# A two-layer block on one core: the first group's work first, token normalisation on ScalarE, and a planner that counts changes of use of TensorE's array

## The chip, the cores and the metric

The kernel runs on one core of one Trainium2 chip. The core has five engines with their own instruction streams: TensorE (PE in the profile, with its weight loads as PEld), VectorE (DVE), ScalarE (ACT), GpSimd (POOL) and SyncE (SP), which issues the transfers. The metric is the device time of one execution in microseconds (us), taken as the median of the runs shown.

## The reference

Input x is 8 x 512 tokens of 256 values. Everything is float32. The first layer is

```python
xn = layernorm(x)                                   # over 256, eps 1e-5
x = x + attention(xn) + experts(xn)
```

with, for 16 heads of 64,

```python
q, k, v = rmsnorm(xn @ Wq) * qw, rmsnorm(xn @ Wk) * kw, xn @ Wv
gate = softplus(einsum(k, u / norm(u)) / 8)                      # one number per key and head
bias = -max(i - j, 0) * softplus(omega) * slope * gate[j]        # causal: -inf for j > i
y = softmax(q @ k.T / 8 + bias) @ v @ Wproj
```

and an expert layer in which each of 32 experts chooses 8 of the 512 tokens of a batch row (softmax over the tokens, top 8), merges them by their weights, applies 257 -> 1024 -> gelu -> 1025 -> 256, and adds the result back to its tokens. The second layer is

```python
xn = layernorm(x)
x = x + gelu(xn @ W_K.T @ W1.T) @ W2.T + ffn(xn)    # ffn: router picks 4 of 16 blocks of 64, relu
```

## The kernel before

**Work.** Attention runs in 32 groups (8 batch rows x 4 sets of four heads). A group is made by `produce(n)`: for each of four token tiles of 128, `project` computes q and k together (`q_k`, L597, 128x512 out), the values with four columns that give the gate's logit (`val`, L605, 260 columns), the square, sum and inverse root for the norm (L612, L629, L205), the scaled rows (L639) and their transposes (L655, L660, L667). After the fourth tile `gate` computes the softplus by a series of some 17 small VectorE steps (L698 to L710), splits the result into three bf16 parts on GpSimd (L730 to L751) and transposes it (L768, L775). Then eight units `attend(u)` run on the group: a unit is a pair of heads and one tile of query rows. Its `scores` (L807, L811) contract over 64 rows, so that two heads stand in the two halves of the array; then come the maximum (L820), the exponential (L828), the inverse (L835), the division on GpSimd (L838), the transposes (L851) with their copies (L859, L861), and after four units the `values` (L885), which use the array in two column halves. `output` (L915) multiplies a batch row's finished heads by Wproj. `expert` works on 4 experts at a time, in column quarters of the array (L992, L1052). `second` is the second layer, which runs for 8 batch rows at the end.

**Start.** `norm_rows(b)` loads a batch row of tokens, takes mean and variance (L408, L410), the inverse root on GpSimd (L414), normalises (L417), and transposes (L425) into `xnT`. Row 0 goes in four tiles, the others whole. `masks` and `bias_rows` (L236, L244) write two constant arrays on GpSimd that every score needs. `gate_weights(g)` (L340) multiplies Wk by the normalised vectors u of a set of heads, which gives the four extra columns of `val`. `choose` picks the experts' tokens for four batch rows. All loads stand on SyncE's queue.

**The order.** The program is written as a list of operations (`op`), each with its engine, an estimated cost in ns, what it depends on, a due time (`prio`, in units of attention: unit u is due at u) and counted buffers that it takes and gives back (`acq`, `rel`): two score buffers `sc`, two projection buffers `mm`, two transpose buffers `tr`, and so on. `Plan.emit` (L67) simulates the engines with these costs and writes out each engine's instructions in the order that it finds. On every engine it takes, among the operations due within the next 12 units, the first in due time that can start now, or else the one that can start earliest. An operation on TensorE has a `mode`, its use of the array: F (whole), R (two row halves: scores), C (two column halves: values), E (column quarters: experts), G and Q (small ones). The plan adds 93 ns where the mode differs from the last (L113); the mode has no part in the choice. The order is fixed when the program is built; on the chip the engines only wait for each other's semaphores.

```python
                    if ok and (pick is None or start < pick[0] - 1e-6):
                        pick = (start, o)
                        if start <= free[e]:
                            break
```

Of the kernel before, what the change touches and what calls it, by code (L numbers as in the profile page):

```python
# [15 lines left out]
P = 128  # L16
# [32 lines left out]
class Plan:  # L49
# [3 lines left out]
    SWITCH = 93  # L53
# [13 lines left out]
    def emit(self):  # L67
# [13 lines left out]
        while left:  # L81
# [4 lines left out]
            for e, ops in ready.items():  # L86
                pick = None
                for o in ops:
# [15 lines left out]
                    if ok and (pick is None or start < pick[0] - 1e-6):  # L104
                        pick = (start, o)
                        if start <= free[e]:
                            break
                if pick and (best is None or pick[0] < best[0]):
                    best = pick
            start, o = best  # L110
            cost = o.cost
            if o.eng == "PE":
                cost += self.SWITCH * (o.mode != mode)  # L113
                mode = o.mode
# [21 lines left out]
    AHEAD = 12.0  # L136


@with_exitstack
def tile_two_layer_block(  # L140
# [82 lines left out]
    with tc.tile_pool(name="pb", bufs=2) as pb, tc.tile_pool(name="pb1", bufs=1) as pb1:  # L223
# [20 lines left out]
        def bias_rows():  # L244
            nc.gpsimd.iota(bst, pattern=[[0, NPR], [1, T]], base=-MID, channel_multiplier=0,
                           allow_small_or_imprecise_dtypes=True)

            for h in range(2):
                k = slice(h * D, (h + 1) * D)
                for q in range(NPR):  # L250
                    r0 = 2 * NSP * q
                    for first, fill in ((r0 + NSP, 1.0), (r0 + 2 * NSP, 0.0)):
                        nc.gpsimd.affine_select(
                            out=bst[k, q, :], in_=bst[k, q, :], compare_op=ALU.is_ge, fill=fill,
                            base=first - 1, pattern=[[0, T]], channel_multiplier=-1,
                        )
                    if q:
                        nc.gpsimd.affine_select(
                            out=bst[k, q, :], in_=bst[k, q, :], compare_op=ALU.is_ge, fill=0.0,
                            base=-r0, pattern=[[0, T]], channel_multiplier=1,  # L260
                        )

        consts = [op("POOL", 2000, masks, (), -8.0), op("POOL", 5500, bias_rows, (), -7.0)]
        zeros = op("POOL", 2000, lambda: nc.gpsimd.memset(mT, 0.0), (), 4.0)

        def load(dst, src, prio, cost=60, acq=()):
            return op("DMA", cost, lambda: nc.sync.dma_start(dst, src), (), prio, acq=acq, lat=2000)
# [3 lines left out]
        for g in range(NHG):  # L271
            at = -18.0 if g == 0 else -9.0 + g
            w_qk[g], w_v[g] = [], []
            heads = slice(g * GW, (g + 1) * GW)
            for dc in range(NC):
                rows = slice(dc * P, (dc + 1) * P)
                w_qk[g].append(load(wqk_sb[:, dc, g, GW:], wk[rows, heads], at, 655))
            for dc in range(NC):
                rows = slice(dc * P, (dc + 1) * P)
                w_qk[g].append(load(wqk_sb[:, dc, g, :GW], wq[rows, heads], at + 0.1, 655))  # L280
                w_v[g].append(load(wvg_sb[:, dc, g, :GW], wv[rows, heads], at + 0.2, 655))
# [4 lines left out]
            load(w128[h * D : (h + 1) * D, k : k + 1], r.unsqueeze(1), -15.5)  # L286
# [34 lines left out]
        for k, f in enumerate(log1p_steps(lambda: oz, lambda: oy, lambda: oy2, lambda: om_sb)):  # L321
# [12 lines left out]
        v_u = [  # L334
            load(ub, u.rearrange("h d -> (h d)").partition_broadcast(P), -19.0, 600, acq=["eh"]),
            load(kwb, k_rms_w.partition_broadcast(P), -18.9, acq=["gT"]),
        ]
        w_g = {}

        def gate_weights(g, at):  # L340
            m = Grp()
            mine = ub3[:, g * HG : (g + 1) * HG, :]
            wide = lambda k: wqk_sb[:, k, g, GW:].rearrange("p (h d) -> p h d", d=D)

            def squares():
                m.sq = pb.tile([P, 2 * HG, D], F32, tag="sq", name=f"usq_{g}", bufs=1)
                nc.vector.tensor_mul(m.sq[:, :HG], mine, mine)

            def norms():
                m.un = pb.tile([P, HG], F32, tag="un", name=f"un_{g}")  # L350
                nc.vector.tensor_reduce(m.un, m.sq[:, :HG], AX.X, ALU.add)

            def floor():
                nc.vector.tensor_scalar(m.un, m.un, U_EPS, None, ALU.max)

            d = [op("DVE", 334, squares, v_u, at, acq=["sq"])]
            d = [op("DVE", 334, norms, d, at + 0.01)]
            d = [op("POOL", 1030, lambda: nc.gpsimd.tensor_tensor(m.un, m.un, phalf, ALU.pow),
                    d, at + 0.02)]
            d = [op("DVE", 86, floor, d, at + 0.03)]  # L360
            d = [op("DVE", 86, lambda: nc.vector.reciprocal(m.un, m.un), d, at + 0.04)]
            d = [op("DVE", 334, lambda: nc.vector.tensor_mul(
                mine, mine, m.un.unsqueeze(2).to_broadcast([P, HG, D])), d, at + 0.05)]
            d = [op("DVE", 334, lambda: nc.vector.tensor_mul(
                mine, mine, kwb.unsqueeze(1).to_broadcast([P, HG, D])), d, at + 0.06)]
            done = []
            for dc in range(NC):
                a = op("DVE", 334, lambda dc=dc: nc.vector.tensor_mul(
                    m.sq[:, dc * HG : (dc + 1) * HG], wide(dc), mine), d + w_qk[g], at + 0.07)
# [706 lines left out]
        for n in range(NIT):  # L1076
            produce(n)
            for k in range(NU):
                attend(n * NU + k)
# [531 lines left out]
```

## Time and profile before

| | us |
|---|---|
| median of 3 runs (1490.54 to 1491.31) | 1491.2 |
| the profiled execution | 1489.48 |
| its span, first to last instruction | 1487.8 |
| first score (L807) | 63.45 |
| last score | 1202 |
| TensorE idle in the span | 57.0 |
| ScalarE on exponentials (L828) | 284.2 |
| GpSimd on divisions (L838) | 266.2 |

The first 63 us bring in tokens and weights and make the first group; up to about 1204 us attention, outputs and experts share the engines; then the second layer follows. A group of instructions is named by its line, its engine and what it writes and reads; `x4` is a count. A releaser in brackets, such as `<-DVE x L417`, is what ended the engine's idle time just before. A matmul's duration includes the filling of the array, which overlaps the next one, so the distance of two starts says what it costs.

### The profile page before, as it was taken

The page shows a single profiled execution, that of the slowest core. Times are in us where ns is not written, and L with a number is a line of the kernel's source. Part 1 is how long each engine was busy: PE and PEld are TensorE (multiplying, and loading weights), DVE is VectorE, ACT ScalarE, POOL GpSimd, SP SyncE. Part 2 cuts the span into 40 slices and gives each one's busy share as a digit, 9 for nine tenths or more (in the row PEclk, how much of TensorE's full clock was granted, in tenths as well). Part 3 has the DMA queues.
Part 4 walks back from the last instruction along what each step waited for, and adds up shares of the span by engine and source line. Part 5 has one row for each costly group of instructions (what it writes and reads, how often), then busy time and mean ns, then how long its engine had stood idle before and what let it go on. Part 6 is the DMA issues. An engine that isn't in the chain of part 4 may idle for free.

```text
span 1487.8 us, 25107 instructions
## 1 busy us (share of the span) xinstructions
PE 1430.8 (96%) x8317; PEld 866.3 (58%) x8332; DVE 906.4 (61%) x3461; ACT 715.0 (48%) x1928; POOL 600.4 (40%) x1109
## 2 busy tenths in 40 slices
PE   3999999999999999999999999999999899999999
PEld 1555556556655665566556655665566466566666
DVE  6888776676677667766776677667766632322210
ACT  1455555555555556555655565655554531222221
POOL 5544554454454345444454454445444421111100
PEclk9999999999999999999999999999999999999999
DMA  6010111232231321232132213122220000000000
GB/s 203 4 57 1 61 61 60 73 111 65 81 102 59 103 85 57 63 105 80 58 118 65 65 62 114 65 69 85 79 74 9 1 15 15 11 18 15 19 15 22
DMA packets 74688, 90.19 MB, mean 61 GB/s; under 512 B 5800, under 2 KB 57760, under 8 KB 74560
## 3 DMA queue, kind: packets, MB, share of 16 engines
q1 hardware_dynamic: 74560, 88.59, 18.4%
q8 instruction: 67, 1.10, 0.3%
q14 instruction: 61, 0.50, 0.1%
HBM read 84.11 MB, written 4.19 MB: 59 GB/s over the span
## 4 chain that ended last, share of the span: by engine, by line
PE 86%; DVE 8%; ACT 3%; issue 1%; POOL 1%; DMA 1%; SPq 0%; ACTq 0%; DVEq 0%; POOLq 0%
PE pq L597 14%; PE pp L851 9%; PE y L885 8%; PE sc L811 8%; PE ph L1497 8%; PE py L1544 7%; PE po L915 7%; PE pv L605 7%; PE pqk L655 4%; PE sc L807 4%; PE peo L1052 2%; PE ph L992 2%; DVE pr L820 1%; ACT pr L828 1%; DVE ss L629 1%
## 5 line engine op out<-in xcount | busy, mean ns | idle before, releaser
L838 POOL TENSOR_SCALAR pr<-pr,rinv 128x384 f32<-128x384 f32 (+3 forms) x512 | 266.2, 533 | 324.9 <-DVE rinv L835 243.2
L828 ACT ACTIVATE pr<-pr,nm 128x384 f32<-128x384 f32 (+3 forms) x512 | 284.2, 557 | 112.6 <-DVE nm L820 72.8
L205 POOL TENSOR_TENSOR rsqk<-ss,nhalf 128x8 f32<-128x8 f32 x128 | 210.6, 1646 | 218.2 <-DVE ss L632 199.0
L820 DVE CUSTOM_DVE_ANT_0 pr<-sc,later 128x384 f32<-128x384 f32 (+3 forms) x512 | 238.8, 483 | 39.1 <-PE sc L811 35.7
L597 PE MATMUL pq<-wqk_sb,xnT 128*128 128x512 f32 x512 | 248.4, 608 | 2.6 <-DVE gl L623 2.6
L851 PE MATMUL pp<-ident,pr 128*128 128x128 f32 x1280 | 220.0, 282 | 10.6 <-POOL pr L838 2.8
L851 PEld LDWEIGHTS pp<-ident,pr 128*128 128x128 f32 x1280 | 149.7, 141 | 128.6 <-issue 67.8
L811 PE MATMUL sc<-kT,qT 64*128 64x384 f32 (+3 forms) x1024 | 181.9, 437 | 0.0
L859 ACT COPY prT<-pp 128x384 f32<-128x384 f32 (+3 forms) x256 | 107.6, 423 | 147.3 <-PE pp L851 146.4
L861 DVE COPY prT<-pp 128x384 f32<-128x384 f32 (+3 forms) x256 | 124.2, 486 | 72.1 <-PE pp L851 68.4
L885 PE MATMUL y<-prT,v 128*64 128x512 f32 (+3 forms) x1024 | 152.9, 439 | 2.2 <-ACT prT L859 1.8
L605 PE MATMUL pv<-wvg_sb,xnT 128*128 128x260 f32 x512 | 138.3, 393 | 2.3 <-DVE tm L639 2.3
L597 PEld LDWEIGHTS pq<-wqk_sb,xnT 128*128 128x128 f32 x512 | 88.5, 193 | 78.2 <-issue 67.1
L612 ACT ACTIVATE sq<-pq 128x512 f32<-128x512 f32 x128 | 76.2, 595 | 113.9 <-PE pq L597 98.9
L885 PEld LDWEIGHTS y<-prT,v 128*64 128x64 f32 x1024 | 69.1, 136 | 96.4 <-issue 65.3
L1497 PE MATMUL ph<-xT,mT 128*128 128x512 f32 x256 | 121.1, 595 | 0.6 <-DVE nm L820 0.2
L915 PE MATMUL po<-wp_sb,yT 128*128 128x256 f32 x512 | 116.1, 380 | 0.1
L629 DVE TENSOR_REDUCE ss<-sq 128x8 f32<-128x512 f32 x128 | 87.0, 680 | 37.8 <-ACT sq L612 37.5
L605 PEld LDWEIGHTS pv<-wvg_sb,xnT 128*128 128x128 f32 x512 | 89.6, 192 | 32.3 <-issue 9.4
L639 DVE TENSOR_TENSOR tm<-pq,rsqk 128x512 f32<-128x512 f32 x128 | 87.8, 686 | 31.7 <-POOL rsqk L205 30.8
L915 PEld LDWEIGHTS po<-wp_sb,yT 128*128 128x128 f32 x512 | 95.1, 190 | 13.0 <-issue 0.3
L1552 DVE TENSOR_TENSOR ot<-py,x 128x256 f32<-128x256 f32 x32 | 13.6, 424 | 143.7 <-PE py L1544 143.7
(259 smaller groups left out, 1885.4 us busy)
## 6 DMA issues: line engine op xcount, KB each, us to landing
ew<-in_L_ffn_w_dram SPq DMA_DIRECT2D x128, 512.0 KB
xr<-in_L_attn_x_dram SPq DMA_DIRECT2D x32, 128.0 KB
out_dram<-ot SPq DMA_DIRECT2D x32, 128.0 KB
x<-in_L_attn_x_dram SPq DMA_DIRECT2D x7, 512.0 KB
raw<-in_L_ffn_w_dram SPq DMA_DIRECT2D x4, 512.0 KB
wqk_sb<-in_L_attn_Wk_dram SPq DMA_DIRECT2D x8, 128.0 KB
wqk_sb<-in_L_attn_Wq_dram SPq DMA_DIRECT2D x8, 128.0 KB
wvg_sb<-in_L_attn_Wv_dram SPq DMA_DIRECT2D x8, 128.0 KB
```

The lines of the kernel that those rows point to most:

```text
L205: nc.gpsimd.tensor_tensor(r, src, nhalf[:, :n], ALU.pow)
L597: nc.tensor.matmul(s.pq[t], xnT[b][:, dc, cols], wqk_sb[:, dc, g, :], start=(dc == 0), stop=(dc == NC - 1),)
L605: nc.tensor.matmul(s.pv[t][:, : GW + HG], xnT[b][:, dc, cols], wvg_sb[:, dc, g, :], start=(dc == 0), stop=(dc == NC - 1),)
L811: nc.tensor.matmul(m.sc[:, h, :w], s.qT[k, q, n0:w], s.kT[k, q, :w], start=False, stop=True)
L820: nc.vector.tensor_tensor_reduce(m.p[:, h, :], m.sc[:, h, :w], later[:, T - w :], -1.0, BIG, ALU.add, ALU.min, m.nm[:, h : h + 1],)
L828: nc.scalar.activation(m.p[:, h, :], m.p[:, h, :], AF.Exp, bias=m.nm[:, h : h + 1], scale=-1.0, accum_out=m.sums[:, h : h + 1],)
L838: nc.gpsimd.tensor_scalar(m.p[:, h, :], m.p[:, h, :], m.rinv[:, h : h + 1], 1.0, ALU.mult, ALU.mult)
L851: nc.tensor.transpose(m.pt[h][:, d * P : (d + 1) * P], m.p[:, h, j * P : (j + 1) * P], ident)
L861: nc.vector.tensor_copy(dst, src)
L885: nc.tensor.matmul(pp.yp[h * D : (h + 1) * D, j * P :], s.v[j][:, hh * D : (hh + 1) * D], pp.tri[:, h, j : j + 4 * (NT - 1 - j) + 1 : 4, : ...
L915: nc.tensor.matmul(o.po[:, :C], yT[b * nk + k][:, t * P : (t + 1) * P], wp_sb[:, k, :], start=(k == 0), stop=(k == nk - 1),)
L1497: nc.tensor.matmul(m.ph[:, i, :], w1T[:, dc, k * P : (k + 1) * P], s.xT[:, dc, :], start=(dc == 0), stop=False,)
```

## The change

Six things change.

1. **The choice on TensorE.** `choose` in the plan takes, among the TensorE operations that can start at the earliest possible moment, the one with the least due time, after these shifts: one unit earlier for an operation with the mode in use, and for any other partial use after a partial use; one unit later for a score (R) after whole-array work when fewer than two R operations could start. The price of a changed mode is 96 ns, and 57 or 104 ns more on a return to the whole array (the second for an operation above 700 ns with the first price).
2. **First group first.** Wk, Wq and Wv of the first set of heads are loaded as whole transfers and early; Wv, u and the key norm's weights of this set go out on ScalarE's queue, and u is loaded by sets. An operation `begun`, which emits nothing, depends on everything that the first group's scores need; the other sets' gate weights, the statistics of batch rows 1 to 7 and the gate matrix of `choose` depend on it. The first group's q and k of two tiles use the score buffers, and its values the transpose buffers.
3. **Constants.** `bias_rows` no longer selects rows in 128x512 on GpSimd: two small tables of row scales are made there, and ScalarE writes each of the two arrays with one activation. Masks and tables come after the first roots. Zeroing of `mT` is cut in eight.
4. **Gate weights.** The square is ScalarE's, both halves of Wk are multiplied and summed in one step each, and the inverse norm is applied to the 8 results and not to u.
5. **Normalised tokens.** For batch rows 1 to 7 ScalarE applies scale and bias (28 steps of 128x256), with a bias that VectorE makes in one small step per row. Row 0 stays on VectorE.
6. **Due times and costs.** Rows 1 to 7 and `choose` are due later and further apart, experts start two groups of units later and follow each other in 6 instead of 6.5 units a quarter, and some estimated costs change (relu 675 for 485, q's copy 462 for 362, k's 394 for 334, the gate's 335 for 598).

```diff
     LAT = {"PE": 220, "DVE": 140, "ACT": 140, "POOL": 90, "DMA": 0}
-    SWITCH = 93
+    SWITCH = 96
+    SECOND = 57, 104
...
                 pick = None
+                able = []
...
-                    if ok and (pick is None or start < pick[0] - 1e-6):
+                    if ok and e != "PE" and (pick is None or start < pick[0] - 1e-6):
                         pick = (start, o)
                         if start <= free[e]:
                             break
+                    if ok and e == "PE":
+                        able.append((start, o))
+                if able:
+                    pick = self.choose(able, free[e], mode)
                 if pick and (best is None or pick[0] < best[0]):
                     best = pick
             start, o = best
             cost = o.cost
             if o.eng == "PE":
-                cost += self.SWITCH * (o.mode != mode)
+                if o.mode != mode:
+                    cost += self.SWITCH
+                    if o.mode == "F":
+                        cost += self.SECOND[cost > 700]
                 mode = o.mode
...
+    SAME, OTHER, ALONE = 1.0, 1.0, 1.0
+    def choose(self, able, free, mode):
+        now = max(free, min(s for s, _ in able))
+        can = [o for s, o in able if s <= now + 1e-6]
+        alone = mode == "F" and sum(o.mode == "R" for o in can) < 2
+        def due(o):
+            if o.mode == mode:
+                return o.prio - self.SAME
+            if "F" not in (o.mode, mode):
+                return o.prio - self.OTHER
+            return o.prio + self.ALONE * (alone and o.mode == "R")
+        best = min(can, key=due)
+        return now, best
...
+        pos = pb.tile([P, T], F32, tag="pr1", name="pos", bufs=1)
...
+        def row_scales():
+            nc.gpsimd.iota(pos, pattern=[[1, T]], base=-MID, channel_multiplier=0,
                            allow_small_or_imprecise_dtypes=True)
...
+        def bias_rows(q):
+            nc.scalar.activation(
+                bst[:, q, :], pos, AF.Identity, bias=rows[:, 1, q : q + 1],
+                scale=rows[:, 0, q : q + 1],
+            )
+        zeros = [
+            op("POOL", 270, lambda e=e: nc.gpsimd.memset(mT[:, :, e : e + 4, :], 0.0), (),
+               4.0 + 0.1 * e)
+            for e in range(0, E, 4)
+        ]
+        def load(dst, src, prio, cost=470, acq=(), by="DMA"):
+            go = nc.scalar if by == "ACT" else nc.sync
+            return op(by, 100 if by == "ACT" else cost, lambda: go.dma_start(dst, src), (), prio,
+                      acq=acq, lat=2000 + (cost if by == "ACT" else 0))
...
-            w_qk[g], w_v[g] = [], []
+            at = -23.5 if g == 0 else -9.0 + g
+            by = "ACT" if g == 0 else "DMA"
...
+            w_qk[g] = [
+                load(wqk_sb[:, :, g, GW:], both(wk), at, 900),
+                load(wqk_sb[:, :, g, :GW], both(wq), at + 0.1, 900),
+            ]
+            w_v[g] = [load(wvg_sb[:, :, g, :GW], both(wv), at + 0.2, 900, by=by)]
...
+        v_kw = load(kwb, k_rms_w.partition_broadcast(P), -23.8, acq=["gT"], by="ACT")
+        v_u = {}
+        for g in range(NHG):
+            v_u[g] = [v_kw, load(
+                ub[:, g * GW : (g + 1) * GW],
+                u[g * HG : (g + 1) * HG, :].rearrange("h d -> (h d)").partition_broadcast(P),
+                -23.9 if g == 0 else -9.1 + g, 500, acq=["eh"] if g == 0 else [],
+                by="ACT" if g == 0 else "DMA",
+            )]
         w_g = {}
+        roots = []
+        begun = op("POOL", 1, lambda: None, (), -6.9)
...
+            d = [op("ACT", 272, squares, v_u[g] + ([begun] if g else []), at, acq=["sq"])]
+            s = [op("DVE", 334, lambda: nc.vector.tensor_reduce(
+                m.un, m.sq[:, :HG], AX.X, ALU.add), d, at + 0.01)]
             d = [op("DVE", 334, lambda: nc.vector.tensor_mul(
-                mine, mine, m.un.unsqueeze(2).to_broadcast([P, HG, D])), d, at + 0.05)]
-            d = [op("DVE", 334, lambda: nc.vector.tensor_mul(
-                mine, mine, kwb.unsqueeze(1).to_broadcast([P, HG, D])), d, at + 0.06)]
-            done = []
-            for dc in range(NC):
-                a = op("DVE", 334, lambda dc=dc: nc.vector.tensor_mul(
-                    m.sq[:, dc * HG : (dc + 1) * HG], wide(dc), mine), d + w_qk[g], at + 0.07)
-                done.append(op("DVE", 334, lambda dc=dc: nc.vector.tensor_reduce(
-                    wvg_sb[:, dc, g, GW:], m.sq[:, dc * HG : (dc + 1) * HG], AX.X, ALU.add),
-                    [a], at + 0.08))
-            w_g[g] = done + [op("DVE", 1, lambda: None, done, at + 0.09,
-                                rel=["sq"] + (["eh", "gT"] if g == NHG - 1 else []))]
+                mine, mine, kwb.unsqueeze(1).to_broadcast([P, HG, D])), d, at + 0.015)]
+            r = [op("POOL", 1030, lambda: nc.gpsimd.tensor_tensor(m.un, m.un, phalf, ALU.pow),
+                    s, at + 0.02)]
+            roots.extend(r)
+            r = [op("DVE", 86, lambda: nc.vector.tensor_scalar(m.un, m.un, U_EPS, None, ALU.max),
+                    r, at + 0.03)]
+            r = [op("DVE", 86, lambda: nc.vector.reciprocal(m.un, m.un), r, at + 0.04)]
+            d = [op("DVE", 598, products, d + s + w_qk[g][:1], at + 0.07)]
+            d = [op("DVE", 598, lambda: nc.vector.tensor_reduce(
+                m.gw.rearrange("p k h -> p (k h)"), m.sq, AX.X, ALU.add), d, at + 0.08)]
+            w_g[g] = [op("DVE", 86, lambda: nc.vector.tensor_mul(
...
-            gate_weights(g, -17.0 if g == 0 else -3.0 + 2 * g)
+            gate_weights(g, -15.95 if g == 0 else -3.0 + 2 * g)
...
-                            [ld], a_)
+                            [ld] + ([begun] if b else []), a_)
...
+                if b == 0:
+                    roots.append(rs)
+                else:
+                    nb = op("DVE", 86, lambda t0=t0, t1=t1: nc.vector.scalar_tensor_tensor(
+                        m.ve[:, t0:t1], m.mv[:, t0:t1, 0], -1.0, m.rs[:, t0:t1],
+                        ALU.mult, ALU.mult), [rs], a_ + 0.04)
                 for t in ts:
-                    xn = op("DVE", 334, lambda t=t: nc.vector.tensor_scalar(
-                        m.x[:, t, :], m.x[:, t, :], m.mv[:, t, 0:1], m.rs[:, t : t + 1],
-                        ALU.subtract, ALU.mult), [rs], a_ + 0.1)
+                    if b:
+                        xn = op("ACT", 370, lambda t=t: nc.scalar.activation(
+                            m.x[:, t, :], m.x[:, t, :], AF.Identity, bias=m.ve[:, t : t + 1],
+                            scale=m.rs[:, t : t + 1]), [nb], a_ + 0.1)
+                    else:
+                        xn = op("DVE", 334, lambda t=t: nc.vector.tensor_scalar(
+                            m.x[:, t, :], m.x[:, t, :], m.mv[:, t, 0:1], m.rs[:, t : t + 1],
+                            ALU.subtract, ALU.mult), [rs], a_ + 0.1)
...
-        tg = op("PE", 150, turn_gw, [v_g], 4.0, acq=["tr"], mode="G")
+        tg = op("PE", 150, turn_gw, [v_g, begun], 4.0, acq=["tr"], mode="G")
...
+        first = roots[:1] + roots[-NT:]
+        consts = [op("POOL", 1000, masks, first, -8.0)]
+        sc_ = op("POOL", 2000, row_scales, first, -7.9, acq=["pr1"])
+        for q in range(NPR):
+            consts.append(op("ACT", 485, lambda q=q: bias_rows(q), [sc_], -7.0,
+                             rel=["pr1"] if q == NPR - 1 else []))
         for b in range(1, BPG):
-            norm_rows(b, 2.0 * b, [list(range(NT))])
-        choose(0, 8.0)
+            norm_rows(b, 5.0 * b, [list(range(NT))])
+        choose(0, 19.0)
         for b in range(BPG, B):
-            norm_rows(b, 10.0 + 2.0 * (b - BPG), [list(range(NT))])
-        choose(1, 18.5)
+            norm_rows(b, 21.0 + 4.0 * (b - BPG), [list(range(NT))])
+        choose(1, 38.0)
...
+                qk_in = "sc" if n == 0 and t < 2 else "mm"
+                v_in = "mm" if n else "tr"
...
-                a = op("PE", 1716, q_k, x_T[b] + w_qk[g], at + w, acq=["mm"])
+                a = op("PE", 1716, q_k, x_T[b] + w_qk[g] + vals[-2:-1], at + w,
+                       acq=[qk_in])
                 projected.append(a)
-                v = op("PE", 876, val, x_T[b] + w_v[g] + w_g[g], at + w + 0.01, acq=["mm"])
+                v = op("PE", 876, val, x_T[b] + w_v[g] + w_g[g], at + w + 0.01, acq=[v_in])
+                vals.append(v)
...
+            if n == 0:
+                begun.deps += grp[0].ready
...
-        step = (NIT - NHG - 2) * NU / (4 * NG)
+        step = (NIT - NHG - 4) * NU / (4 * NG)
         for g in range(NG):
-            h0, h1, d0, d1 = (NHG * NU + step * (4 * g + k) + 0.7 for k in range(4))
+            h0, h1, d0, d1 = ((NHG + 2) * NU + step * (4 * g + k) + 0.7 for k in range(4))
...
-                    hid.append(op("ACT", 485, lambda i=i, f=relu: f(i),
+                    hid.append(op("ACT", 675, lambda i=i, f=relu: f(i),
```

## What the change does to the time: a prediction

> **What bounds the kernel now.** I read the page's first part, then the chain of waits, then the busy time by stage, and last TensorE's own timeline.
>
> ```profile
> PE 1430.8 (96%) x8317; PEld 866.3 (58%) x8332; DVE 906.4 (61%) x3461; ACT 715.0 (48%) x1928; POOL 600.4 (40%) x1109
> ...
> PE 86%; DVE 8%; ACT 3%; issue 1%; POOL 1%; DMA 1%; SPq 0%; ACTq 0%; DVEq 0%; POOLq 0%
> ```
>
> TensorE is the bound: 1430.8 of 1487.8 us busy, and 86% of the chain that ended last. So only two things can shorten the run: TensorE's idle time (57.0 us) and time inside its "busy" that does no work. By stage (columns: length, then busy time and count of PE, PEld, DVE, ACT, POOL; clock; DMA share; GB/s):
>
> ```profile
> 0.00:63.45 63.45, 35.41 (x118) 19.99 (x119) 47.17 (x178) 13.52 (x31) 32.92 (x70) 0.92 0.41 122
> 63.45:200.00 136.55, 130.90 (x830) 74.80 (x831) 109.75 (x431) 77.38 (x229) 70.37 (x128) 0.99 0.13 43
> 200.00:1200.00 1000.00, 985.76 (x6126) 588.84 (x6128) 682.03 (x2583) 558.88 (x1563) 470.66 (x878) 1.00 0.22 72
> 1200.00:1487.80 287.80, 278.71 (x1249) 182.63 (x1258) 67.47 (x274) 65.26 (x108) 26.46 (x34) 0.99 0.05 17
> ```
>
> Idle: 28.0 us before the first score at 63.45, then 5.7, 14.2 and 9.1. Half of all idle time is in the first 4% of the run. No other engine passes 80% of a long stage after that.
>
> The start, from the timelines of GpSimd, VectorE and TensorE:
>
> ```profile
> 7.99 2.61 POOL L253 TENSOR_SCALAR_AFFINE_SELECT bst<-bst 64x512 bf16<-64x512 bf16 x4
> 11.36 1.02 POOL L358 TENSOR_TENSOR un<-un,phalf 128x4 f32<-128x4 f32 x1
> 12.36 2.08 POOL L414 TENSOR_TENSOR ars<-ave,nhalf 128x1 f32<-128x1 f32 x4
> 16.39 1.34 PE L425 MATMUL pxT<-ident,x 128*128 128x128 f32 x4 [16.39 <-DVE x L417]
> 32.13 0.69 PE L425 MATMUL pxT<-ident,x 128*128 128x128 f32 x2 [4.08 <-DVE x L417]
> 39.73 3.00 PE L597 MATMUL pq<-wqk_sb,xnT 128*128 128x512 f32 x4
> ```
>
> The token roots (L414) stand on GpSimd behind the constant rows, though their input is ready at about 4 us; TensorE first moves at 16.39. Later it waits 4.08 us for tokens of the second batch row, ahead of the first row's own second and third tile.
>
> A steady piece of TensorE's timeline (start, duration; the next start, not the duration, says what a row costs):
>
> ```profile
> 63.45 0.34 PE L807 MATMUL sc<-gT,bst 64*128 64x384 bf16 x2 [0.16 <-DVE gT L775]
> ...
> 64.26 0.23 PE L807 MATMUL sc<-gT,bst 64*128 64x128 bf16 x2
> ...
> 514.78 0.66 PE L851 MATMUL pp<-ident,pr 128*128 128x128 f32 x4
> 515.37 0.34 PE L807 MATMUL sc<-gT,bst 64*128 64x384 bf16 x2
> 515.54 0.81 PE L811 MATMUL sc<-kT,qT 64*128 64x384 f32 x4
> 516.28 0.66 PE L851 MATMUL pp<-ident,pr 128*128 128x128 f32 x4
> 516.77 1.88 PE L597 MATMUL pq<-wqk_sb,xnT 128*128 128x512 f32 x4
> 518.49 1.04 PE L605 MATMUL pv<-wvg_sb,xnT 128*128 128x260 f32 x4
> ...
> 532.25 0.60 PE L851 MATMUL pp<-ident,pr 128*128 128x128 f32 x4
> 532.69 0.64 PE L597 MATMUL pq<-wqk_sb,xnT 128*128 128x512 f32 x1
> ```
>
> Four transposes inside whole-array work take 0.44 (532.25 to 532.69); just after scores 0.49; just after column-tiled work and ahead of scores 0.59 (514.78 to 515.37). A 384-wide score takes 0.81 with another score behind it (63.45 to 64.26), 0.91 with whole-array work behind it. So leaving a use of the array costs 0.10, and coming back to the whole array 0.05 more; ahead of a projection it is 0.10 more (in that timeline pq takes 1.82 us after a score, 1.72 after transposes).
>
> **Part 1, the order (choose, SECOND).** Over the whole TensorE timeline I counted 662 changes of use and 297 returns to the whole array: 662 x 0.097 + 297 x 0.062 (mean of both return prices) = 83 us, 5.6% of the run. The 256 scores stand in 226 visits; only 30 visits hold two. A visit avoided saves 0.10 + 0.10 + 0.06 = 0.26 us. With two score buffers a visit can hold two. Is the second buffer free? A score is issued every 4.45 us (63.45 to 1204 us, 256 of them), and at 500 to 533 us VectorE has read a score 1.5 to 2.5 us after its issue, so both are free half the time; a lone score is held back one unit (4.45 us) while other work is there. The trace shows no order by this rule: bounds are no pair more (0) and all paired (98 visits x 0.26 = 25.5). I take four scores of five paired, 154 visits: 72 x 0.26 = **18.7**. Values and experts enter from the whole array 59 times; put behind a score they save 0.16 each; bounds 0 and 9.4, I take 24, **3.8**. Sum 22.5.
>
> What the moved work costs: a later score makes exponentials, divisions and transposes later, and the VectorE maxima come four in a row (up to 2.8 us by 0.69 us rows). Cover is the ready projections and outputs on TensorE; without it, every pair leaves a wait. That price is a rival below.
>
> The Trainium skill, page "TensorEngine Tiling (Array Packing)", section "Key Properties", says that a change of tiling mode drains the array but not a change of tile; it gives no time, and the 0.10 us above is this case's price. By that rule alone a switch between scores and values should cost as much as any other.
>
> **Part 2, the start.** First tokens land at 2.95 and their variances are ready at 3.97, as now. With the constant rows (7.6 us of GpSimd, 3.69 to 11.27) behind the roots: root 0.5, normalise 0.4, transpose 0.7, copy 0.4: first tile at 6.2. Weights: x 0.52, Wk, Wq, Wv 0.26 each, u 0.13, together 1.4 MB, at 167 GB/s (0 to 16.39 us) 8.6, at 253 GB/s (16.39 to 31.78) plus 2 us of latency 7.7; take 8. Then four tiles of 1.72 + 0.88 = 10.4, transposes between them 1.7, cold clock 2.7: 22.8 for the last tile, pq ending 0.9 earlier. Its square, sum, mean, root and gate scale are 0.60 + 0.68 + 0.17 + 1.65 + 0.17 = 3.3, 25.5 with hand-overs. The gate: 17 small VectorE steps 3.2, Exp 0.2, eight GpSimd steps 2.2, transpose 0.4, copy 0.4, hand-overs 0.8: 7.2. First score at 33 instead of 63.45. Bounds: 28 (no cold clock, no hand-overs), 38 (the gate as slow as now, 51.64 to 63.45).
>
> TensorE's useful work by then: 10.4 + token transposes 1.1 + q/k transposes 1.8 + 0.2 + two tiles ahead 3.4 = 16.9, so 16.1 us lost. Before: 28.0 idle and 6.3 of slow matmuls (pq 3.62 and 3.00 against 1.88, and five shorter rows), 34.3. Gain 18.2. Given back: the deferred gate weights and tokens meet the first scores on VectorE, and the pipeline fills with little else: between 0 and 10 (twice the 5.7 of 63 to 200), take 4.5. Net **13.5**, bounds 3 and 23.
>
> The clock row first: after the 4.08 us wait, slice 30 to 40 us had a granted clock of 0.59 and pq took 3.00. The page "TensorE: Matmul & The Clock Gate", section "What's actually happening", says that idling one window of about 3.4 us halves the clock until a busy window. By it the wait for the gate, which is new here ahead of the first score, brings one more cold window: 1.7 us, an estimate from that page; the sum would be 34.3 for 36. It speaks against the change.
>
> Against loads on ScalarE's queue the page "DMA: Bandwidth & Descriptors", section "Issuing engines are not separate DMA queues", says that only issue time is saved. The rows' 167 and 253 GB/s from one queue fit it.
>
> **Part 3, the rest.** Normalised tokens: 28 VectorE steps of 0.44 go (12 us), 7 of 0.17 come; ScalarE gets 28 of about 0.47 (the nearest row, L660, scaled 128x256; 0.37 by the plain copy) = 13 us. Cover: ScalarE is 52% idle and rows 1 to 7 have 19 units or more until use; without cover the loss is 28 x 0.03. Identity at L500 runs with no table load. The two bias-row steps on ScalarE (0.68 each by L500) and split zeroing lie before or beside scores: 0. Omega, norm weights and the later groups' loads are moved behind the first on SP; they are due after 9 us: 0. The tail from 1200 us: scores' rule also delays the 16 start steps; costs for relu are nearer the rows (0.68). Idle there is 9.1, so between -5 and +5; 0.
>
> **Sum.** 22.5 + 13.5 = 36.0. The profiled execution took 1489.48 (span 1487.8), 1.7 below the median 1491.2. 1489.5 - 36.0 = 1453.5, plus 1.7: **1455**.
>
> **Rivals.**
> 1. Few new pairs: one buffer is usually still held when a score falls due, and the one-unit delay rarely decides. Against: the 2 us hold in 4.45. Order gain 7, start 13.5: 1471.
> 2. The start gives it back: VectorE, 74% busy in the first 63 us, makes up the deferred work later and TensorE idles 10 instead of 4.5 us, with the first score at 38: start gain 3, order 22.5: 1466.
> 3. All pairs and joins come, first score at 28: 25.5 + 9.4 + 21: 1435.
> 4. Slower: pairs starve TensorE. For: transposes already wait up to 2.48 us for a division, and two transpose buffers serve scores, tokens, q/k and values. Place: the transposes (L851) after each pair. It decides from 36.0 / 128 = 0.28 us a pair; at 0.37 it costs 47: 1502. Against: 14.2 us idle in 1000 now, with work of twelve units to choose from.
>
> **How the numbers follow.** Chances: forecast 0.60 (1441 to 1466), few pairs 0.13, start given back 0.08, everything 0.07, slower 0.10, and 0.02 for effects that cancel. Range 1434 to 1483: the low end is rival 3, the high end an order gain of 6 and a start gain of 3. Runs of this kernel spread by 0.8 us, so 0.2% (3 us) is the bound for no change: faster 0.86, same 0.03, slower 0.11.
>
> **What would show it.** After: first score near 33 us; TensorE idle before it near 13; scores in about 154 visits; TensorE busy near 1405; idle in the attention stage still near 15 per 1000. Wrong if visits stay above 200, if the first score is later than 40, or if idle time ahead of L851 rises from 10.6 to over 40.

## The result and the profile after

The changed kernel took 1464.49 us (median of 4 runs, 1463.22 to 1464.89) against 1490.87 before: ratio 0.9828, 95% interval 0.9815 to 0.9841. It is 26.4 us faster; 36 were forecast. Over all comparisons single runs of the kernel before lie between 1486.3 and 1491.9 us, with medians from 1489.1 to 1490.9, so a difference of 2 or 3 us between kernels that were timed in different rounds is not certain. The page after, first part and chain:

```profile
PE 1414.9 (97%) x8332; PEld 866.3 (59%) x8332; DVE 888.8 (61%) x3428; ACT 735.0 (50%) x1961; POOL 595.7 (41%) x1115
...
PE 85%; DVE 7%; ACT 5%; issue 1%; POOL 1%; DMA 1%; ACTq 0%; SPq 0%; DVEq 0%; POOLq 0%
```

TensorE is busy for 15.9 us less with the same matmuls, and idle for 48.3 us instead of 57.0. By stage, with the same columns as above:

```profile
0.00:41.73 41.73, 23.05 (x76) 12.84 (x77) 23.57 (x91) 12.30 (x25) 22.05 (x70) 0.97 0.60 181
41.73:200.00 158.27, 151.32 (x908) 90.62 (x909) 129.56 (x531) 104.86 (x298) 86.76 (x146) 0.98 0.05 16
200.00:1200.00 1000.00, 984.18 (x6233) 599.00 (x6230) 677.99 (x2578) 562.63 (x1550) 467.01 (x874) 0.99 0.24 76
1200.00:1463.20 263.20, 256.34 (x1119) 163.86 (x1117) 57.63 (x231) 55.26 (x88) 19.88 (x25) 1.00 0.05 17
```

The first score starts at 41.73 instead of 63.45, with 18.7 us of idle time before it instead of 28.0. In the attention stage TensorE idles 15.8 us per 1000 instead of 14.2. TensorE's start:

```profile
10.04 1.11 PE L489 MATMUL pxT<-ident,x 128*128 128x128 f32 x4 [10.04 <-DMA w<-in_L_attn_q_rms_w_dram]
12.81 1.35 PE L489 MATMUL pxT<-ident,x 128*128 128x128 f32 x4 [1.65 <-issue]
13.95 3.62 PE L673 MATMUL pq<-wqk_sb,xnT 128*128 128x512 f32 x4
...
35.50 0.63 PE L731 MATMUL pqk<-ident,tm 128*128 128x128 f32 x4 [1.49 <-DVE gp L357]
39.24 1.08 PE L731 MATMUL pqk<-ident,tm 128*128 128x128 f32 x4 [3.12 <-DVE tm L715]
...
41.73 0.51 PE L886 MATMUL sc<-gT,bst 64*128 64x384 bf16 x2 [0.64 <-DVE gT L854]
42.00 1.51 PE L890 MATMUL sc<-kT,qT 64*128 64x384 f32 x4
```

The first projection (L673) starts at 13.95, behind the transposes of all four tiles. Before the first score TensorE waits for the gate, and the score then takes 1.51 us; 0.82 is usual. A pair of the changed order, at full clock:

```profile
53.93 0.28 PE L886 MATMUL sc<-gT,bst 64*128 64x256 bf16 x2
54.05 0.60 PE L890 MATMUL sc<-kT,qT 64*128 64x256 f32 x4
54.49 0.33 PE L886 MATMUL sc<-gT,bst 64*128 64x384 bf16 x2
```

Two scores follow each other, and the 256-wide one costs 0.56 (53.93 to 54.49) where a lone one took 0.65 before.

### The profile page after: what moved, and what is told of

It is laid out like the page before. It is cut to its first block, busy times and chain, and to the rows that moved or that the text cites. A ratio compares the mean times of both kernels' runs of the same rounds, so it can differ in the third digit from the quotient of the medians.

```text
span 1463.2 us, 25079 instructions
## 1 busy us (share of the span) xinstructions
PE 1414.9 (97%) x8332; PEld 866.3 (59%) x8332; DVE 888.8 (61%) x3428; ACT 735.0 (50%) x1961; POOL 595.7 (41%) x1115
## 4 chain that ended last, share of the span: by engine, by line
PE 85%; DVE 7%; ACT 5%; issue 1%; POOL 1%; DMA 1%; ACTq 0%; SPq 0%; DVEq 0%; POOLq 0%
PE pq L673 13%; PE pp L930 10%; PE sc L890 8%; PE y L964 8%; PE ph L1578 8%; PE po L994 8%; PE py L1625 7%; PE pv L681 7%; PE pqk L731 3%; PE sc L886 3%; PE peo L1131 2%; PE ph L1071 2%; ACT pr L907 2%; DVE pr L899 2%; PE ph L1582 1%
## 5 line engine op out<-in xcount | busy, mean ns | idle before, releaser
L907 ACT ACTIVATE pr<-pr,nm 128x384 f32<-128x384 f32 (+3 forms) x512 | 284.6, 557 | 142.6 <-DVE nm L899 116.1
L673 PE MATMUL pq<-wqk_sb,xnT 128*128 128x512 f32 x512 | 245.2, 602 | 0.3 <-DVE gl L699 0.2
L930 PEld LDWEIGHTS pp<-ident,pr 128*128 128x128 f32 x1280 | 151.2, 141 | 133.0 <-issue 78.8
L930 PE MATMUL pp<-ident,pr 128*128 128x128 f32 x1280 | 219.3, 281 | 10.7 <-POOL pr L917 3.4
L964 PE MATMUL y<-prT,v 128*64 128x512 f32 (+3 forms) x1024 | 154.1, 444 | 2.0 <-DVE kT L743 1.2
L673 PEld LDWEIGHTS pq<-wqk_sb,xnT 128*128 128x128 f32 x512 | 88.4, 192 | 73.1 <-issue 62.2
L964 PEld LDWEIGHTS y<-prT,v 128*64 128x64 f32 x1024 | 68.4, 138 | 95.7 <-issue 66.3
L1633 DVE TENSOR_TENSOR ot<-py,x 128x256 f32<-128x256 f32 x32 | 13.5, 423 | 157.6 <-PE py L1625 157.6
L715 DVE TENSOR_TENSOR tm<-pq,rsqk 128x512 f32<-128x512 f32 x128 | 87.9, 686 | 21.8 <-POOL rsqk L234 20.6
```

The lines of the kernel that those rows point to most:

```text
L673: nc.tensor.matmul(s.pq[t], xnT[b][:, dc, cols], wqk_sb[:, dc, g, :], start=(dc == 0), stop=(dc == NC - 1),)
L907: nc.scalar.activation(m.p[:, h, :], m.p[:, h, :], AF.Exp, bias=m.nm[:, h : h + 1], scale=-1.0, accum_out=m.sums[:, h : h + 1],)
L930: nc.tensor.transpose(m.pt[h][:, d * P : (d + 1) * P], m.p[:, h, j * P : (j + 1) * P], ident)
L964: nc.tensor.matmul(pp.yp[h * D : (h + 1) * D, j * P :], s.v[j][:, hh * D : (hh + 1) * D], pp.tri[:, h, j : j + 4 * (NT - 1 - j) + 1 : 4, : ...
```

## Experiments

Each kernel is the changed one with one edit, except `order_only`. "Changes" and "returns" are changes of use of the array and returns to the whole array, counted in each built program (before 658 and 296, changed 536 and 212; the trace of before, used in the prediction, gave 662 and 297). "Priced" is 0.097 us a change and 0.062 a return. Busy and idle are TensorE's in the profiled execution, which is one run and not always near the median: it took 1486.8 us for `start_only`, 1477.4 for `order_only`, 1478.3 for `same3` and 1475.1 for `partial1_whole3`.

| kernel | median us | ratio to before, 95% | visits of two scores | changes, returns | priced | busy | idle |
|---|---|---|---|---|---|---|---|
| before | 1490.9 | | 30 | 658, 296 | 82.2 | 1430.8 | 57.0 |
| changed | 1464.5 | 0.9815 to 0.9841 | 69 | 536, 212 | 65.1 | 1414.9 | 48.3 |
| order_only | 1480.3 | 0.9919 to 0.9943 | 68 | 530, 209 | 64.4 | 1415.0 | 60.7 |
| start_only | 1482.1 | 0.9944 to 0.9972 | 31 | 646, 289 | 80.6 | 1430.3 | 54.6 |
| norm_dve | 1466.1 | 0.9827 to 0.9853 | 67 | 538, 212 | 65.3 | 1413.8 | 49.9 |
| same3 | 1481.7 | 0.9926 to 0.9954 | 106 | 457, 172 | 55.0 | 1412.2 | 64.3 |
| partial0_whole1 | 1480.0 | 0.9933 to 0.9961 | 26 | 594, 227 | 71.7 | 1419.0 | 58.2 |
| partial1_whole0 | 1490.5 | 0.9997 to 1.0017 | 51 | 604, 262 | 74.8 | 1425.4 | 61.2 |
| partial3_whole1 | 1460.4 | 0.9798 to 0.9828 | 113 | 475, 196 | 58.2 | 1405.1 | 54.3 |
| partial1_whole3 | 1472.9 | 0.9876 to 0.9912 | 69 | 515, 192 | 61.9 | 1417.1 | 56.2 |
| own_tile | 1461.1 | 0.9801 to 0.9829 | 69 | 536, 212 | 65.1 | 1410.8 | 48.1 |
| no_gating | 1460.6 | 0.9800 to 0.9828 | 66 | 543, 216 | 66.1 | 1411.9 | 47.0 |
| old_due | 1470.6 | 0.9863 to 0.9892 | 64 | 538, 213 | 65.4 | 1415.2 | 52.2 |
| partial3_own_tile | 1458.0 | 0.9780 to 0.9808 | 113 | 475, 196 | 58.2 | 1404.6 | 52.0 |

### The order alone, and the rest alone

`order_only` is the kernel before with the new class `Plan`; `start_only` is the changed kernel with the old one.

```diff
 class Plan:
-    SWITCH = 93
+    SWITCH = 96
+    SECOND = 57, 104
...
+                if able:
+                    pick = self.choose(able, free[e], mode)
```

> The kernel before with the new choice and prices on TensorE alone. Its program has 530 changes of use and 209 returns to the whole array, before 658 and 296. Theory 1 (each change costs 0.097 us and each return 0.062 on the path): 128 x 0.097 + 87 x 0.062 = 17.8 us faster than before, about 1473; the start stays as before (first score near 63 us). Theory 2 (changes of use are hidden; the gain came from the start and the due times): within 3 us of before, 1488 to 1494. Theory 3 (pairing starves TensorE of transposes and only the start pays): slower than before.

> The changed kernel with the choice and the price of the kernel before, all else as changed. 646 changes and 289 returns, the changed kernel 536 and 212. Theory 1: 110 x 0.097 + 77 x 0.062 = 15.4 us slower than the changed kernel, about 1480; so the start, the due times and the rest are worth some 11 of 26 us. Theory 2: within 3 us of the changed kernel's 1464.5. Theory 3: faster than the changed kernel.

The order alone brings 10 us (1490.3 to 1480.3, the medians of that comparison), less than theory 1's 17.8; TensorE's busy time falls by 15.8, near its price, but its idle time rises by 3.7. Taking the order out of the changed kernel costs 17.6 us by the medians, a little more than the 15.4 of theory 1; the profiled run of `start_only`, 4.7 us above its median, has 15.4 more busy and 6.3 more idle. So theories 2 and 3 fall, and theory 1 comes near in one of the two kernels. The new prices were not tried apart from the new choice. The rest alone brings 8.2. The two alone make 18.2 of 26.4; 8 us come only with both.

### Keeping a use

```diff
-    SAME, OTHER, ALONE = 1.0, 1.0, 1.0
+    SAME, OTHER, ALONE = 3.0, 1.0, 1.0
```

> The changed kernel with the bonus for the use in force raised from 1 unit to 3 (SAME 3, OTHER 1, ALONE 1): 106 visits hold two scores instead of 69, 41 one instead of 118; 457 changes and 172 returns instead of 536 and 212. Theory 1: 79 x 0.097 + 40 x 0.062 = 10.1 us faster than the changed kernel, 1454 to 1455. Theory 3 (more pairs starve TensorE): not faster than 1464, and idle time of TensorE between 200 and 1200 us above 25 instead of 15.8.

17 us slower than the changed kernel, though it makes 79 changes fewer. In 200 to 1200 us TensorE idles 29.3 us instead of 15.8:

```profile
200.00:1200.00 1000.00, 970.74 (x6181) 597.42 (x6180) 671.38 (x2553) 550.22 (x1541) 464.99 (x870) 1.00 0.23 76
```

This fits theory 3. But SAME does two things: it keeps scores together, and it holds scores back behind whole-array work. The next four kernels set the two apart:

```diff
             if o.mode == mode:
-                return o.prio - self.SAME
+                return o.prio - (3 if mode != "F" else 1)
```

with the pairs (0, 1), (1, 0), (3, 1) and (1, 3) for a partial use and the whole array.

> The changed kernel with its bonus split by the use in force: none for staying in a partial use, 1 unit for staying with the whole array (so a score is only held back, and two are no longer kept together). 594 changes, 227 returns, 26 visits of two scores. Theory 1 (the count of changes sets the gain: start_only with 646 and 289 took 1482.1): 52 x 0.097 + 62 x 0.062 = 8.9 us faster than that, 1473. Theory 4 (holding scores back behind ready whole-array work is itself the gain, the pairs are by the way): 1463 to 1468.

> The other half: 1 unit for staying in a partial use, none for staying with the whole array. 604 changes, 262 returns, 51 visits of two scores. Theory 1: 42 x 0.097 + 27 x 0.062 = 5.7 us faster than start_only, 1476. Theory 4: no gain over start_only, 1480 to 1490.

> 3 units for staying in a partial use, 1 for the whole array: 113 visits of two scores (69 in the changed kernel), 475 changes, 196 returns (536, 212). Theory 1: 61 x 0.097 + 16 x 0.062 = 6.9 us faster than the changed kernel, 1457 to 1458. Theory 3 (pairs starve TensorE, as same3's 1481.7 may say): 1472 or more, and idle of TensorE in 200 to 1000 us near same3's 17.8 instead of 7.6. Theory 5 (same3 lost by staying too long with the whole array, pairs are harmless): 1457 to 1464.

> 1 unit for staying in a partial use, 3 for the whole array: 69 visits of two scores as in the changed kernel, 515 changes, 192 returns. Theory 1: 21 x 0.097 + 20 x 0.062 = 3.3 us faster than the changed kernel, 1461. Theory 5: slow like same3, 1475 or more. Theory 3: near the changed kernel, 1460 to 1466, since the pairs are the same.

`partial3_whole1` has more pairs than `same3` and is the fastest of the five. Its pairs cost some idle time in this stage (20.6 us for 15.8) and save more busy time (9.8 us over the run), so theory 3 falls. With 3 units for the whole array instead of 1 the kernel is slower twice (`same3` against `partial3_whole1`, `partial1_whole3` against the changed kernel), as theory 5 says, though its 1475 or more for the latter was missed. Its stage, then that of `partial1_whole3`, which has the changed kernel's pairs but stays long with the whole array:

```profile
200.00:1200.00 1000.00, 979.43 (x6249) 606.01 (x6249) 684.30 (x2574) 550.88 (x1547) 464.10 (x872) 1.00 0.23 76
```

```profile
200.00:1200.00 1000.00, 976.88 (x6184) 593.83 (x6182) 672.52 (x2569) 571.30 (x1554) 467.07 (x863) 0.99 0.23 75
```

20.6 and 23.1 us idle. The last is 8.4 us slower than the changed kernel where its count made it 3.3 faster.

The trace of `partial1_whole3` shows where: 10.4 of the 23.1 us are four waits of 2.61 us ahead of values. ScalarE has a table to load whenever it goes from the exponential (L907) to the experts' gelu (L1098) or back, 1.28 us each time. The plan counts one such load for the two gelu steps of an expert stage (`586 + 1283 * (1 - half)`). In the changed kernel the two stand together; here an exponential stands between them, which makes four loads instead of two, and the copy that the values need comes late:

```profile
402.45 1.28 ACT L1098 ACT_TABLE_LOAD   x1
403.74 1.15 ACT L1098 ACTIVATE ehT<-ehT 128x512 f32<-128x512 f32 x2
405.13 1.28 ACT L907 ACT_TABLE_LOAD   x1 [0.24 <-DVE nm L899]
```

```profile
397.44 0.63 ACT L1098 ACTIVATE ehT<-ehT 128x512 f32<-128x512 f32 x1
398.08 1.28 ACT L907 ACT_TABLE_LOAD   x1
...
399.87 1.28 ACT L1098 ACT_TABLE_LOAD   x1
401.17 0.63 ACT L1098 ACTIVATE ehT<-ehT 128x512 f32<-128x512 f32 x1
401.70 0.35 ACT L938 COPY prT<-pp 128x256 f32<-128x256 f32 x1
402.11 3.88 PE L964 MATMUL y<-prT,v 128*64 128x512 f32 x16 [2.61 <-ACT prT L938]
```

So the loss in this kernel is in large part ScalarE's order, and not, as theory 5 says, an array kept too long in one use. The two gelu steps are split in four expert stages here and in `partial0_whole1`, in two in `same3`, `order_only` and `old_due` (below), and in none of the others. No kernel that only joins them was run.

The two halves of the bonus alone gave 1480.0 and 1490.5, against 1464.5 with both and 1482.1 for `start_only`, which also lacks OTHER, ALONE and the new prices. The first fails theories 1 and 4; the second has no gain over `start_only`, as theory 4 says, with 42 changes fewer: its busy time is 4.9 us less, its idle time 6.6 more, and by the medians it is 8.4 us slower. So the unit for the whole array is needed, and three are too many: with 1 unit for a partial use 0, 1 and 3 give 1490.5, 1464.5 and 1472.9. OTHER was never varied. Theory 1 holds for the busy time and not for the time: in twelve of the fourteen kernels busy less priced lies between 1345.7 and 1350.6 us. The two with 3 units for the whole array are at 1357.2 and 1355.2; in `partial1_whole3` the granted clock was 0.50 from 402.8 to 406.2, after the wait shown, and 0.98 in each of the four 100 us stretches that have such a wait, which accounts for some of it. For `same3` the cause stays open.

### Tokens on ScalarE

```diff
-                else:
+                elif False:
...
-                    if b:
+                    if False:
                         xn = op("ACT", 370, ...
```

> The changed kernel with the tokens of rows 1 to 7 normalised on VectorE again (28 steps of 128x256), all else as changed; 538 changes and 212 returns. Theory 1 (no engine but TensorE is on the path, the move is free): 1464 to 1466. Rival (VectorE is close to the path between 42 and 200 us, and the 12 us taken from it are felt): 1468 to 1476, with more idle time of TensorE before 200 us than 25.6.

1466.1, 1.6 us more by the medians; the intervals of the ratios overlap. Idle before 200 us was 26.8 against 25.6. The move is at best worth a microsecond or two. A step on ScalarE took 0.53 us (14.7 us for 28).

### What makes the start

```diff
-                a = op("PE", 1716, q_k, x_T[b] + w_qk[g] + vals[-2:-1], at + w,
+                own = x_T[b][t : t + 1] if n == 0 else x_T[b]
+                a = op("PE", 1716, q_k, own + w_qk[g] + vals[-2:-1], at + w,
...
-                v = op("PE", 876, val, x_T[b] + w_v[g] + w_g[g], at + w + 0.01, acq=[v_in])
+                v = op("PE", 876, val, own + w_v[g] + w_g[g], at + w + 0.01, acq=[v_in])
```

> The changed kernel, in which the first group's q, k and values of a token tile depend on that tile's tokens alone (x_T[b][t]) and not on all four. TensorE's first projection then stands ahead of the transposes of tiles 2 and 3; the 536 changes and everything after the first score keep their order. Theory A (the list's dependency on four tiles held the first projection, 11.2 against 13.95 us, and so the first score at 41.7): first score near 39, 2 to 3 us faster than the changed kernel, 1461.5 to 1462.5. Rival (the first score hangs on the roots and the gate, not on the first projection): first score 41 to 42, 1464.

Theory A holds for the first score. In `own_tile` the projection moves up, and the first score with it:

```profile
10.44 1.11 PE L489 MATMUL pxT<-ident,x 128*128 128x128 f32 x4 [10.44 <-DVE x L481]
11.64 3.10 PE L673 MATMUL pq<-wqk_sb,xnT 128*128 128x512 f32 x4
...
38.25 0.50 PE L887 MATMUL sc<-gT,bst 64*128 64x384 bf16 x2 [0.65 <-DVE gT L855]
```

The kernel is 3.4 us faster by the medians (1461.1), 1.9 by the ratios to the kernel before; the intervals of the ratios overlap, so that the gain is likely and its size not sure.

```diff
-            if n == 0:
-                begun.deps += grp[0].ready
```

> The changed kernel without the dependence of the later gate weights, batch rows and gate matrix on the first group (begun depends on nothing); loads, roots, constants, due times and the choice on TensorE as changed. 543 changes, 216 returns. Theory S (the deferral makes the early first score, and that is most of the 8 us that the rest of the change brings): first score after 50 us, 1470 to 1473. Rival (work done earlier is not needed later, the deferral only moves it): 1463 to 1467.

Both theories miss: the first score comes at 46.24, not after 50, and the kernel is not slower: 3.9 us faster than the changed one by the medians, 2.1 by the ratios, whose intervals overlap. Up to 46.24, without the deferral and then with it (changed kernel):

```profile
0.00:46.24 46.24, 29.07 (x102) 16.98 (x103) 34.50 (x133) 16.90 (x37) 27.68 (x74) 0.96 0.54 167
```

```profile
0.00:46.24 46.24, 26.75 (x94) 15.28 (x96) 27.52 (x107) 13.79 (x30) 23.16 (x71) 0.92 0.54 164
```

Without it TensorE has done 2.3 us more by then, at a higher clock, and VectorE 7 us more. The early first score is bought with engines that stand still while the gate's chain of small steps runs.

```diff
-            norm_rows(b, 5.0 * b, [list(range(NT))])
-        choose(0, 19.0)
+            norm_rows(b, 2.0 * b, [list(range(NT))])
+        choose(0, 8.0)
...
-            norm_rows(b, 21.0 + 4.0 * (b - BPG), [list(range(NT))])
-        choose(1, 38.0)
+            norm_rows(b, 10.0 + 2.0 * (b - BPG), [list(range(NT))])
+        choose(1, 18.5)
...
-        step = (NIT - NHG - 4) * NU / (4 * NG)
+        step = (NIT - NHG - 2) * NU / (4 * NG)
...
-            h0, h1, d0, d1 = ((NHG + 2) * NU + step * (4 * g + k) + 0.7 for k in range(4))
+            h0, h1, d0, d1 = (NHG * NU + step * (4 * g + k) + 0.7 for k in range(4))
```

> The changed kernel with the due times of before for batch rows 1 to 7, for the experts' choice and for the experts (steps of 6.5 units, two groups earlier); 538 changes, 213 returns. Theory 1 (due times of this work are no part of the gain): 1463 to 1466. Rival (VectorE and ScalarE are pressed by it while attention fills, 42 to 200 us): 1468 or more, TensorE idle in 41.7 to 200 us above 10 instead of 7.0.

1470.6: the due times are worth 6.1 us, as the rival has it, but its sign is just missed: from 41.7 to 200 us TensorE idles 9.5 us, not above 10, where the changed kernel has 7.0. From the first score on:

```profile
40.23:200.00 159.77, 150.25 (x933) 85.92 (x933) 127.37 (x511) 102.21 (x290) 82.83 (x141) 0.98 0.12 42
```

Over the whole run TensorE idles 3.9 us more (52.2 for 48.3). The idle time ahead of values (L964, L914 in `order_only`) is 2.0 us in the changed kernel; in `old_due` and in `order_only`, the two kernels that join the new order to the old due times, it is:

```profile
L964 PE MATMUL y<-prT,v 128*64 128x512 f32 (+3 forms) x1024 | 157.3, 451 | 8.1 <-ACT prT L938 7.1
L914 PE MATMUL y<-prT,v 128*64 128x512 f32 (+3 forms) x1024 | 155.5, 447 | 6.4 <-ACT prT L888 6.2
```

Most of it are two waits of 3.30 us in the one and of 2.97 in the other, each at an expert stage whose gelu steps an exponential divides. The kernel before, with the same due times and the old order, has 2.2. So part of the 8 us that come only with both is seen here: with the old due times the new order meets these table loads, with the new ones it doesn't. The rest of them stays open, and the old choice with the old due times and the new start was not run.

### The version that beats both

> partial3_whole1 (1460.4) together with own_tile's edit. If the two are independent: 1460.4 less what own_tile gains, 1457.5 to 1458.5 by theory A. By its rival 1460.

1458.0 us, ratio 0.9794 (0.9780 to 0.9808): as expected, and just clear of the changed kernel's interval. It joins `partial3_whole1` and `own_tile`. `no_gating` was not tried with them.

## Why the prediction was right or wrong

**The total came near by some luck.** 1464.5 lies within the forecast's 1441 to 1466, but the sum took its two parts as independent. Alone they bring 10.0 and 8.2 us for the 22.5 and 13.5 forecast; the 8 us that come only with both were in no term.

**The price of a change of use was right.** 0.097 and 0.062 us from neighbouring rows carry the busy time of twelve kernels within 5 us. "72 x 0.26 = 18.7" failed in its 72: "I take four scores of five paired" should have been 138 of 256, in 187 visits instead of 154. The reason that the prediction gave, "a lone score is held back one unit (4.45 us) while other work is there", fails twice. Built with ALONE 0 or 4 the program has 534 or 537 changes: the rule hardly moves the count (neither was run). In the list of choices as the program is built, 121 of the 151 visits that come from the whole array (or a small use) start when no whole-array operation can start, so there is nothing to hold the score back for; and of the 84 that end with one score, 65 have a second one counted as able, which then lacks a buffer, loses to whole-array work by due time, or stands behind values or experts. `partial3_whole1`, with 113 visits of two, shows that the pairs were to be had.

**"Joins" (3.8) is in the same sum.** Entries to values and experts from the whole array fell from 59 to 46, by 13 where 24 were taken. Together the order was forecast at 22.5; priced it is 17.1, busy time gave 15.9, and undoing it costs 17.6.

**The cover was wrong, the rival that rests on it too.** "With work of twelve units to choose from" TensorE has little that can start. Rival 4 named pairs as what starves it; `partial3_whole1`, with most pairs, has 12.0 us of idle time before the transposes (L930) for the changed kernel's 10.7, so pairs alone don't. The place was right in part: in `same3` it is 19.2 us. In `partial1_whole3` it is 10.1, and the loss stands before the values (10.8 for 2.0).

**The start: 13.5 forecast, 8.2 measured for all but the order**, and 6.1 of the changed kernel's gain hang on due times that were costed at 0. "No other engine passes 80% of a long stage" overlooked VectorE, busy for 109.75 of 136.55 us after the first score. (18.2 less 4.5 is 13.7, not 13.5.) Three steps failed. "First score at 33": it was 41.73, past the 40 that the prediction named as a sign of being wrong. First tokens were read at 4.54, not 2.95 (loads on ScalarE's queue now go out beside them from 0.78; whether that is why was not tried), and the first tile was transposed at 10.04, not by 6; and "take 8" for the first projection overlooked that it depends on four tiles, which `own_tile` prices at 1.9 to 3.4 us. The gate took 10.1 us (31.62 to 41.73) for 7.2. For 1.6 of the 2.9 the next group's root stands in its way on GpSimd, and steps of the next group's norm stand among its own on VectorE:

```profile
36.74 1.64 POOL L234 TENSOR_TENSOR rsqk<-ss,nhalf 128x8 f32<-128x8 f32 x1 [2.11 <-DVE xg L789]
38.34 0.21 POOL L809 TENSOR_TENSOR xg<-xg,cj 128x16 f32<-128x16 f32 x1
```

And the time of the first score was the wrong thing to forecast by: `no_gating` has it later and is no slower. What the load order, the earlier roots and the shorter gate weights each bring to the 8.2 was not taken apart.

**The cold clock came as warned.** The sentence on the page "TensorE: Matmul & The Clock Gate", section "What's actually happening", fits in kind: after the waits for the gate (1.49 and 3.12 us, in the lines above) the granted clock was 0.82 between 41.73 and 63.45, and scores took 1.51 and 1.94 for 0.82 and 1.02. Its size does not fit: no single wait is as long as the page's window of about 3.4 us, and the granted clock was 0.52 from 40 to 50, longer than the one window that the prediction priced at 1.7. The hoped-for gain in slow matmuls did not come: busy less priced is 1348.6 before and 1349.8 after.

**The rest** (tokens on ScalarE, constants) at 0 is right within 1.6 us for the tokens; the constants were not tried by themselves.

## What to carry to other kernels

Where TensorE works in several tilings, price a change of use from neighbouring starts and count the changes: that gives the busy time. It does not give the time, for a new order of TensorE is also a new order of the engines that feed it; here some orders put an exponential between two gelu steps, and TensorE waited about 3 us each time for ScalarE's tables. So look in each trace for what ends TensorE's longest waits, and try the size of a bonus: for the whole array 0, 1 and 3 units gave 1490.5, 1464.5 and 1472.9 us. At the start count the work that the bounding engine has done by a given time, not when the first step of the main loop begins.

## What was not expected of the hardware

The price per change is the same in all directions among whole, row-split and column-split use (from 0.09 to 0.105 us where a direction occurs more than ten times between the two halves and the whole array), and only a return to the whole array costs more: 0.055 us ahead of transposes and 0.10 ahead of projections (four transposes from start to next start take 0.437 us after whole-array work and 0.492 after scores, a projection 1.72 and 1.82). Fourteen orders of the same matmuls let one read it: 1405 to 1431 us of busy time, of which 55 to 82 us are changes by this price.
